# A transformer block on one core: where the shift of the attention scores stands in TensorE's order

## The chip, the cores and the metric

The kernel runs on one core of one Trainium2 chip. The metric is the device time of the whole program in microseconds (us). The engines are named as in the profile: PE (TensorE, matrix products), PEld (its weight loads), DVE (VectorE), ACT (ScalarE), POOL (GpSimd) and SP (SyncE, which only issues DMAs here).

## The reference

For a batch of 4 sequences of 2048 tokens with 512 features, the block normalises x and adds two branches to it, all in float32:

```
xn  = layernorm(x)
out = x + attention(xn) + ffn(xn)

attention: 16 heads of 32;  softmax(q k^T / sqrt(32)) v, then a projection
ffn:       the top 2 of 8 experts per sequence, chosen from token 0;
           mean over the two of  gelu(xn W1 + b1) W2 + b2
```

What matters here is the attention. For every head the scores are a 2048x2048 matrix. The softmax needs the largest score of each query, so that the exponential can be taken of score minus maximum.

## The kernel before, in words

**The unit of work.** Four heads (one group, `GH = 4`) stand beside each other on the 128 partitions: head j has its 32 features on partitions 32j to 32j+31. Work goes in units `U`, one for each combination of a sequence, a group of heads, a chunk of 512 queries (`qc`) and a tile of 128 keys (`kt`): 4 x 4 x 4 x 16 = 1024 units. Each unit makes transposed scores (128 keys by 512 queries) of the four heads.

**Two passes.** The maxima must be known before the exponentials. So the loop at lines 1044 to 1171 carries two passes at once: for unit U the second pass (shift, score, exponential, product with v), and for unit U + 22 (`LEAD`) the first pass, which computes the scores once more in the other orientation, for the maxima alone. The first 22 turns of the loop have only the first pass, the last 22 only the second.

**The products of a unit on PE**, each over 32 partitions (one head), into 128x512 float32, which is one PSUM bank:

- `shift` (lines 912 to 919): a bf16 product of a row of ones with the negated maxima, which stand split into three bf16 parts in `negm`. It starts the accumulation of the bank `s`. The loop calls it for all four heads at once.
- `score` (lines 921 to 928): the float32 product of keys and queries, which is accumulated on top of the shift in the same bank.
- `score_max` (lines 898 to 910): the float32 product of queries and keys for the maxima, into a bank `m`.

Because a product uses 32 of the 128 rows of the array, four products of four different heads (four row groups) can be under way at once. The loop orders the calls so that neighbours belong to different heads: shift 0 to 3, score 0 and 1, maxima 2 and 3, score 2 and 3, maxima 0 and 1. A float32 product is carried out as two passes, each with its own weight load; a bf16 product as one.

**What follows on the other engines.** ACT takes the exponential of the four `s` banks (line 1064) into the tile `p`; DVE takes the maxima of the four `m` banks (line 1071). POOL adds the tiles `p` up for the softmax's denominators (line 966). `p` has five buffers.

**What follows on PE.** After an even unit, `weigh` (line 937) multiplies the exponentials of the two units before with v. After most odd units come products of the dense layers (line 599): queries, keys and values of later groups, the two feed-forward layers, the projection. Which of them stands behind which unit is laid down by `Plan` (lines 41 to 303), together with the loads; some 50 odd units have none. Some units are followed by `add_keys` (line 972), which adds the denominators over the keys. All of these use all 128 rows and 32 columns of the array (`128*32` in the profile), while shift, score and maxima use 32 rows and 128 columns (`32*128`).

**PSUM.** All banks come from one pool of eight, `bank()` at line 345. They are handed out in the order of the program: a new product takes the bank that was asked for longest ago among those given back, and waits until its last reader has finished. Per unit eight banks are asked for, plus one for `acc` after an even unit and one or two for dense products after an odd one.

**The schedule is by hand** (`tc.manual_schedule()`): every engine executes its instructions in the order in which the Python code emits them.

Of the kernel before, what the change touches and what calls it, by code (L numbers as in the profile page):

```python
# [20 lines left out]
GH = P // HD  # L21
# [285 lines left out]
def block_kernel(  # L307
# [37 lines left out]
    def bank(name):  # L345
        return ps.tile([P, CH], F32, tag="bank", name=name)

    def rows_of(j):
        return slice(j * HD, (j + 1) * HD)
# [537 lines left out]
    def place(u):  # L887
        rest, kt = divmod(u, NT)
        rest, qc = divmod(rest, NCH)
        return (*divmod(rest, DC), qc, kt)  # L890
# [7 lines left out]
    def score_max(u, heads, tiles):  # L898

        b, g, qc, n = place(u)  # L900
        i, kc = divmod(n, NCH)
        if n == 0 and (b, g, qc) not in mx:
            mx[b, g, qc] = small.tile([P, GH, TPC, NCH], F32, tag="mx", name=f"mx_{b}_{g}_{qc}")
        for j in heads:
            t = bank(f"m{j}_{u}")
            r = rows_of(j)
            nc.tensor.matmul(  # L907
                t, qT[b, g, qc][r, ts(i, P)], kT[b, g, kc][r, :], start=True, stop=True
            )
            tiles.append((mx[b, g, qc][:, j, i, kc : kc + 1], t))  # L910

    def shift(u, heads, tiles):
        b, g, qc, kt = place(u)
        for j in heads:
            tiles[j] = bank(f"s{j}_{u}")
            r = rows_of(j)
            nc.tensor.matmul(  # L917
                tiles[j], ones_b[r, :], negm[b, g, qc][r, :], start=True, stop=False
            )

    def score(u, heads, tiles):
        b, g, qc, kt = place(u)
        for j in heads:
            r = rows_of(j)
            nc.tensor.matmul(  # L925
                tiles[j], kT[b, g, kt // TPC][r, ts(kt % TPC, P)], qT[b, g, qc][r, :],
                start=False, stop=True,
            )
# [115 lines left out]
    for U in range(-LEAD, plan.units):  # L1044
        second = U >= 0
# [3 lines left out]
        maxima, tiles = [], {}  # L1049


        if second:
            shift(U, range(GH), tiles)
        for h in range(2):
            if second:
                score(U, (2 * h, 2 * h + 1), tiles)
            if first_pass is not None:
                score_max(first_pass, (2 - 2 * h, 3 - 2 * h), maxima)


        if second:
# [111 lines left out]
    U = plan.units  # L1173
# [78 lines left out]
```

## Time and profile before

| | us |
|---|---|
| median of 3 runs (4901.69 to 4907.2) | 4903.32 |
| the profiled execution, device time | 4902.71 |
| its span, first to last instruction | 4900.9 |
| PE busy | 4860.0 (99%) |
| POOL busy | 4504.5 (92%) |
| DVE busy | 3761.9 (77%) |
| ACT busy | 2501.7 (51%) |
| granted TensorE clock, mean | 1.000 |

Three things help in reading it. PE's busy time is the union of products that overlap, and the end of each product is modelled, so 99% doesn't say that the array works at its peak; how far apart the starts of successive products lie says more. In the timeline `x4` joins neighbouring instructions of one kind. And a product can show as `32*128` (32 rows, 128 columns of the array) or `128*32`.

The costliest lines on PE are the products for `s` (line 925, 1926.1 us), `m` (line 907, 1916.8 us), `acc` (line 937, 985.3 us), the dense products (line 599), and the shifts (line 917, 412.7 us).

### The profile page before, as it was taken

Reading aid. Unit: us, or ns where it says so; the run is one execution under the profiler, and the core shown is the slowest. Engines: PE = TensorE matmul, PEld = TensorE weight load, DVE = VectorE, ACT = ScalarE, POOL = GpSimd, SP = SyncE. Lnnn points to the kernel's source line nnn. Section 1 sums busy time; section 2 is a strip of 40 time slices with the busy share of each in tenths; the row PEclk is TensorE's granted clock in tenths of the full one; section 3 lists DMA queues with packets and bytes.
Section 4 is the critical chain, followed back from the end, with each engine's and each line's share of the span. In section 5 each row is a group of like instructions: output and inputs, shape, how many; then the busy total and the mean of one; then the engine's idle time right before and its main releaser. Section 6 shows DMA issues by size and latency. Waiting matters only on the chain.

```text
span 4900.9 us, 112895 instructions
## 1 busy us (share of the span) xinstructions
PE 4860.0 (99%) x46860; PEld 1777.6 (36%) x46860; DVE 3761.9 (77%) x5979; ACT 2501.7 (51%) x4587; POOL 4504.5 (92%) x1524
## 2 busy tenths in 40 slices
PE   8999999999999999999999999999999999999999
PEld 2333333333434333333443443333343334333333
DVE  5777788777777788887777778887777777878772
ACT  1445456554454546564455455555545544555453
POOL 3899999999999998999999999999999999999994
PEclk9999999999999999999999999999999999999999
DMA  6434427654444654765454454476445465323322
GB/s 227 136 99 119 127 87 186 164 157 130 126 129 141 181 144 120 193 171 153 127 156 141 138 160 137 134 198 164 147 130 143 124 174 139 99 77 99 94 72 93
DMA packets 480963, 678.37 MB, mean 138 GB/s; under 512 B 145213, under 2 KB 287549, under 8 KB 463169
## 3 DMA queue, kind: packets, MB, share of 16 engines
q1 hardware_dynamic: 452512, 568.37, 36.5%
q0 software_dynamic: 27936, 102.77, 11.5%
q8 instruction: 369, 6.05, 0.5%
q14 instruction: 146, 1.19, 0.1%
HBM read 437.70 MB, written 193.46 MB: 129 GB/s over the span
## 4 chain that ended last, share of the span: by engine, by line
PE 87%; ACT 6%; POOL 4%; issue 1%; DVE 1%; DMA 1%; SPq 0%; POOLq 0%; DVEq 0%; ACTq 0%
PE acc L937 18%; PE s L925 16%; PE m L907 16%; PE ops L599 7%; PE qkps L599 7%; PE s L917 6%; PE hps L599 6%; PE vps L599 4%; PE prps L599 3%; POOL psum L966 3%; ACT p L1064 3%; PE keys L972 1%; ACT L836 1%; ACT L1068 1%; ACT h L1068 1%
## 5 line engine op out<-in xcount | busy, mean ns | idle before, releaser
L966 POOL TENSOR_TENSOR psum<-psum,p 128x2048 f32<-128x2048 f32 x819 | 3739.0, 4565 | 106.5 <-ACT p L1064 57.5
L1064 ACT ACTIVATE p<-s 128x512 f32<-128x512 f32 x4096 | 2117.9, 602 | 2132.2 <-PE m L907 1923.8
L1071 DVE TENSOR_REDUCE mx<-m 128x1 f32<-128x512 f32 x4096 | 2543.2, 683 | 567.1 <-PE m L907 564.1
L925 PE MATMUL s<-qT,kT 32*128 32x512 f32 x8192 | 1926.1, 587 | 0.0
L907 PE MATMUL m<-kT,qT 32*128 32x512 f32 x8192 | 1916.8, 590 | 0.5 <-DVE sacc L943 0.4
L907 PEld LDWEIGHTS m<-kT,qT 32*128 32x128 f32 x8192 | 923.0, 184 | 330.9 <-issue 240.6
L937 PE MATMUL acc<-p,v 128*32 128x512 f32 x8192 | 985.3, 598 | 16.2 <-ACT p L1064 11.7
L925 PEld LDWEIGHTS s<-qT,kT 32*128 32x128 f32 x8192 | 768.5, 185 | 30.2 <-issue 6.6
L937 PEld LDWEIGHTS acc<-p,v 128*32 128x32 f32 x8192 | 214.1, 109 | 714.7 <-ACT p L1064 402.0
L599 PE MATMUL ops<-wb_w,h 128*32 128x512 f32 x4096 | 466.0, 595 | 0.2 <-ACT p L1064 0.2
L946 DVE TENSOR_TENSOR sacc<-acc,sacc 128x512 f32<-128x512 f32 x448 | 309.8, 692 | 146.0 <-PE acc L937 146.0
L917 PE MATMUL s<-negms,ones_b 32*128 32x512 bf16 x4096 | 412.7, 384 | 6.2 <-ACT sums L984 2.5
L599 PE MATMUL hps<-xt,wt_w 128*32 128x512 f32 x3584 | 411.0, 596 | 0.0
L917 PEld LDWEIGHTS <-ones_b 32*128 32x128 bf16 x4096 | 105.6, 91 | 827.4 <-issue 820.6
L599 PE MATMUL qkps<-xt,wt_qk 128*32 128x512 f32 x3360 | 385.3, 596 | 0.3 <-ACT p L1064 0.3
L960 POOL TENSOR_TENSOR psum<-p,p 128x2048 f32<-128x2048 f32 x63 | 291.7, 4629 | 86.4 <-ACT p L1064 86.2
L599 PEld LDWEIGHTS ops<-wb_w,h 128*32 128x32 f32 x4096 | 120.0, 109 | 327.1 <-issue 229.8
L1087 DVE RECIPROCAL sums<-sums 128x128 f32<-128x128 f32 x252 | 236.1, 937 | 0.0
L599 PEld LDWEIGHTS hps<-xt,wt_w 128*32 128x32 f32 x3584 | 103.3, 109 | 288.6 <-issue 191.2
L801 DVE SCALAR_TENSOR_TENSOR row<-ops,row 128x512 f32<-128x512 f32 x128 | 88.5, 692 | 149.8 <-PE ops L599 143.1
L599 PEld LDWEIGHTS qkps<-xt,wt_qk 128*32 128x32 f32 x3360 | 96.9, 109 | 271.0 <-issue 179.2
L599 PE MATMUL vps<-wt_v,xt 128*32 128x256 f32 x2688 | 153.7, 381 | 0.0
(153 smaller groups left out, 2193.0 us busy)
## 6 DMA issues: line engine op xcount, KB each, us to landing
xt<-t_dram SPq DMA_DIRECT2D x203, 512.0 KB
xt<-xn_dram SPq DMA_DIRECT2D x151, 512.0 KB
psum<-p POOLq DMA_DIRECT2D x62, 1024.0 KB, 8.9
part_dram<-row SPq DMA_DIRECT2D x128, 256.0 KB
wt_w<-ws_dram SPq DMA_DIRECT2D x128, 128.0 KB
v<-v_dram SPq DMA_DIRECT2D x64, 256.0 KB
row<-part_dram SPq DMA_DIRECT2D x64, 256.0 KB
att_dram<-att SPq DMA_DIRECT2D x63, 256.0 KB
```

Of the source, the lines that this page charges most:

```text
L599: nc.tensor.matmul(pp[rows_of(j), :], lhsT[:, rows_of(j)], rhs, start=(first and n == 0), stop=(last and n == len(terms) - 1),)
L907: nc.tensor.matmul(t, qT[b, g, qc][r, ts(i, P)], kT[b, g, kc][r, :], start=True, stop=True)
L917: nc.tensor.matmul(tiles[j], ones_b[r, :], negm[b, g, qc][r, :], start=True, stop=False)
L925: nc.tensor.matmul(tiles[j], kT[b, g, kt // TPC][r, ts(kt % TPC, P)], qT[b, g, qc][r, :], start=False, stop=True,)
L937: nc.tensor.matmul(acc[r, :], held["v", (b, g, kt // TPC)][:, (kt + n) % TPC, r], pT[u + n][:, j, :], start=(n == 0), stop=(n == 1),)
L946: nc.vector.tensor_tensor(t, acc, t, ALU.add)
L960: nc.gpsimd.tensor_tensor(psums[b, g, qc], pT[u - 1], pT[u], ALU.add)
L966: nc.gpsimd.tensor_tensor(psums[b, g, qc], psums[b, g, qc], pT[u], ALU.add)
L1064: nc.scalar.activation(pT[U][:, j, :], tiles[j], AF.Exp, scale=SCALE)
L1068: nc.scalar.activation(flat, flat, AF.Gelu)
L1071: nc.vector.tensor_reduce(dst, t, AX.X, ALU.max, negate=True)
L1087: nc.vector.reciprocal(sums[before][:, q], sums[before][:, q])
```

## The change

The shift is no longer issued for all four heads ahead of the unit's other products. It is issued for two heads at a time: first for heads 0 and 1, then come the maxima products of heads 2 and 3, then the scores of heads 0 and 1; then the shift of heads 2 and 3, the maxima products of heads 0 and 1, and the scores of heads 2 and 3. No instruction is added or taken away on any engine; `shift`, `score` and `score_max` themselves are as they were.

```diff
-        if second:
-            shift(U, range(GH), tiles)
         for h in range(2):
             if second:
-                score(U, (2 * h, 2 * h + 1), tiles)
+                shift(U, (2 * h, 2 * h + 1), tiles)
             if first_pass is not None:
                 score_max(first_pass, (2 - 2 * h, 3 - 2 * h), maxima)
+            if second:
+                score(U, (2 * h, 2 * h + 1), tiles)
```

PE's order in a unit, by head (h shift, s score, m maxima):

```
before   h0 h1 h2 h3   s0 s1  m2 m3   s2 s3  m0 m1
after    h0 h1  m2 m3  s0 s1  h2 h3   m0 m1  s2 s3
```

As the eight banks of a unit are asked for in another order (before: s0 to s3, m2, m3, m0, m1; after: s0, s1, m2, m3, s2, s3, m0, m1), the products take over other banks from their predecessors, and the waits on ACT and DVE stand at other instructions. DVE takes the maxima in the same order of heads as before, 2, 3, 0, 1, and ACT the exponentials of heads 0 to 3.

## The prediction

> **What bounds the kernel now.** I read the page's busy times first, then the chain, then PE's rows among the costliest groups.
>
> ```profile
> PE 4860.0 (99%) x46860; PEld 1777.6 (36%) x46860; DVE 3761.9 (77%) x5979; ACT 2501.7 (51%) x4587; POOL 4504.5 (92%) x1524
> ...
> PE 87%; ACT 6%; POOL 4%; issue 1%; DVE 1%; DMA 1%; SPq 0%; POOLq 0%; DVEq 0%; ACTq 0%
> ...
> L925 PE MATMUL s<-qT,kT 32*128 32x512 f32 x8192 | 1926.1, 587 | 0.0
> ```
>
> PE is the bound: 99% busy, 87% of the chain, next to no idle time before its products. So the time is the sum of what PE's products take one after another, and the question is how a unit's 20 passes fit together. The timeline of one plain unit, with an `acc` behind it, shows that:
>
> ```profile
> 2001.76 0.61 PE L599 MATMUL ops<-wb_w,h 128*32 128x512 f32 x4
> 2002.31 0.40 PE L917 MATMUL s<-negms,ones_b 32*128 32x512 bf16 x4
> 2002.53 0.59 PE L925 MATMUL s<-qT,kT 32*128 32x512 f32 x2
> 2002.54 0.59 PE L907 MATMUL m<-kT,qT 32*128 32x512 f32 x2
> 2002.96 0.59 PE L925 MATMUL s<-qT,kT 32*128 32x512 f32 x2
> ...
> 2003.82 0.59 PE L907 MATMUL m<-kT,qT 32*128 32x512 f32 x2
> 2003.83 0.59 PE L925 MATMUL s<-qT,kT 32*128 32x512 f32 x2
> 2004.35 0.64 PE L937 MATMUL acc<-p,v 128*32 128x512 f32 x4
> ```
>
> Look at the starts. The four shifts start together at 2002.31; 0.22 us later the first passes of two scores and two maxima products start together; each float32 pass then takes 0.43 us (2002.53, 2002.96, ... 2003.82). Four of these steps follow, and 0.52 us after the last starts `acc` begins. From the first shift to `acc`: 0.22 + 3 x 0.43 + 0.52 = 2.04 us. Going through all starts in the trace, 980 of the 1002 units that have both passes stand alone between two `128*32` groups; 834 of them take 2.040 to 2.045 us, and all 980 together 2054.5 us. The other 22 stand in 11 pairs.
>
> Two gaps matter. After 2001.76 the next step would be due at 2002.19 but comes at 2002.31, and `acc` comes 0.09 us after 2003.83 + 0.43: PE empties when it changes between `128*32` and `32*128`. At such a change the weights of the first product cannot be loaded ahead either. What that costs shows in the 22 turns at the start that have maxima products only, so that float32 products come first after the change:
>
> ```profile
> 54.05 1.14 PE L907 MATMUL m<-kT,qT 32*128 32x512 f32 x8
> 55.12 0.64 PE L599 MATMUL vps<-wb_v,xq_stage 128*32 128x512 f32 x4
> ```
>
> Two steps of 0.43 us take 54.05 to 55.12 = 1.07 us: 0.21 us over, of which 0.10 us is the emptying as above. The remaining 0.11 us is the float32 weight load that nothing hides. In the unit at 2002.31 there is no such loss: bf16 shifts come first, the second pass starts after 0.22 us, and the float32 loads run under the shift.
>
> **The change part by part.** Call heads 0 and 1 group A, heads 2 and 3 group B. Group A keeps its order: shift, score, maxima. Group B goes from shift, maxima, score to maxima, shift, score.
>
> Do A and B run independently? In before they march in step, so the change needs it. A unit whose maxima products wait for a bank answers:
>
> ```profile
> 986.62 0.40 PE L917 MATMUL s<-negms,ones_b 32*128 32x512 bf16 x4
> 986.85 0.59 PE L925 MATMUL s<-qT,kT 32*128 32x512 f32 x2
> 987.04 0.70 PE L907 MATMUL m<-kT,qT 32*128 32x512 f32 x2
> 987.28 0.59 PE L925 MATMUL s<-qT,kT 32*128 32x512 f32 x2
> 987.58 0.72 PE L907 MATMUL m<-kT,qT 32*128 32x512 f32 x4
> 988.00 0.59 PE L925 MATMUL s<-qT,kT 32*128 32x512 f32 x2
> ```
>
> Group B's maxima products start 0.19 us late, at 987.04, and their second passes at 987.58; group A goes on at 986.85 and 987.28 undisturbed, and its own maxima products (in the x4) start before s2 and s3 at 988.00, though the program has them after. So the groups run independently and out of program order. The 0.70 against 0.59 is again the open load: 987.04 to 987.58 is 0.54, not 0.43.
>
> Group B's new sequence: maxima first, load open: 0.54, then 0.43; shift; two score passes. For the shift in the middle the trace has a place, too: where two units with scores only stand side by side, four shifts come at 4823.06, in the same mode, and the scores behind them at 4823.27.
>
> ```profile
> 4822.20 1.02 PE L925 MATMUL s<-qT,kT 32*128 32x512 f32 x8
> 4823.06 0.38 PE L917 MATMUL s<-negms,ones_b 32*128 32x512 bf16 x4
> 4823.27 1.02 PE L925 MATMUL s<-qT,kT 32*128 32x512 f32 x8
> ```
>
> Before it 2 x 0.43, the shift itself 0.21 to 0.22, loads hidden on both sides. So B's last pass starts at 0.01 + 0.54 + 0.43 + 0.22 + 0.43 = 1.62 us after the unit's start (before: 1.52), and the unit takes 1.62 + 0.52 = 2.14 us instead of 2.04: +0.10 us. Bounds: 0.09 (shift at 0.21) to 0.11. Group A ends at 1.94, as before, and waits. Over the 980 units, raising all below 2.141 us to that: 834 x 0.10 and a little = +83.5 us.
>
> The Trainium skill speaks against the change more strongly: "TensorE: Matmul & The Clock Gate", Part 3, has matmuls start and end strictly in program order. The rows at 987.58 and 988.00 contradict it. If it held, s0 and s1 could not start before m3's second pass at 0.55 us; A would end about 0.3 us later and the whole would cost some 270 us, an estimate.
>
> The waits that move are all on banks; nothing else on any queue moves, no DMA, nothing on SP's or POOL's queues. The program of after shows which reader each product now waits for.
> (a) `acc` and the dense product waited for the exponential of s0 of the same unit, now for the maximum of m2, which DVE has earlier than 2.14 us. In 57 units a late ACT (a gelu and its table load) held them, at 2.34 us on average; down to 2.141 this gives −11 us.
> (b) 35 units like the one at 986.62 (2.334 us, `keys` directly before): m2 waited for the exponential of s3. Now m0 does, which comes 0.9 us later; m3 waits for the reduce of m0, some 0.05 us. 35 x (2.334 − 2.19) = −5 us.
> (c) The 11 pairs (5.365 us, two units with nothing between): DVE's four maxima take 2.48 us from 1.25 on (1.36 in before). The second unit's shift of head 1 waits for the second of them, 2.55, the shift of head 3 for the fourth, some 3.8; then 0.22 + 0.43 + 0.52, about 5.0 us: −4 us.
> (d) 49 units wait for DVE to free a dense bank for m1 or m0. These now stand ahead of s2 and s3, which wait with them; but the wait ends at the same moment and two float32 steps follow either way: the longer of 2.14 and what they take now, 0.
> The plain unit keeps its cover: in the unit at 2002.31 DVE adds up the dense result (line 801) from 0.13 to 0.82 us after the start, m1's bank is free at 0.88, and m1 and s2 need it at 0.9 to 1.0. If DVE came 0.1 us later, that would cost up to 0.1 us a unit.
>
> POOL (92%) and DVE get 0.1 us more per unit and are not pushed. Sum: 83.5 − 11 − 5 − 4 = +63 us. The profiled execution took 4902.7 us (span 4900.9, 1.8 around it), 0.6 below the median: 4902.7 + 63 = 4966 us. Its own range: 0.09 us a unit and twice the gain on waits, 75 − 40, to 0.11 and no gain, 94: 4938 to 4997.
>
> **The rivals.** More loads open: B's bf16 load and the float32 load of s2 behind it have never run beside float32 passes of the other group in step; the pairs show both hidden, but there all groups are in step. A second open load is another 0.11 us x 834: 4966 + 90 = about 5056. Groups only partly independent (the out-of-order window too short for B's longer queue) would lie above, to 5150. For: two more waits stand ahead of s2. Against: 4823.06. Chance 0.14.
> Faster: PE brings m2's load in before the change of mode is over. Then a unit stays at 2.04 us and only the waits count, down to 2.04: about −16, −10, −5, so 4872. It decides if B's first maxima passes are 0.43 apart instead of 0.54. Against: at 54.05 it is never so. Chance 0.08.
> No change: the load is open but half covered, or the waits gain far more than counted: within 10 us. Chance 0.04.
>
> **How the numbers follow.** Likeliest (0.74): 4966. The range 4940 to 5055 takes in nearly all of it and most of the second-load case; left out are the window too short, no change and faster. Faster or slower is counted from 0.2%, 10 us, about what a measurement can tell: faster 0.08, same 0.04, slower 0.88.
>
> **What would show it.** Right: plain units at 2.14 us; L907's first passes in B at 0.69 instead of 0.59; B's shifts 0.97 us after A's; the mean of L907 up from 590 to about 616 ns (2 of 8 passes by 105 ns); `acc` no longer released by ACT. Wrong: units at 2.04 (load hidden), or at 2.25 and more (a second load open, or m2's passes holding s0 back).

## The result and the profile after

The kernel after takes 4947.07 us (median of 4 runs, 4945.27 to 4949.49) against 4902.5 us before (median of 4 as well): a ratio of 1.0084, 95% interval 1.0072 to 1.0096. It is slower by 0.8%, about 44.6 us, where +63 was forecast; the stated range, 4940 to 5055, holds it. The profiled execution has a span of 4945.5 us.

The page of after, its busy times, its chain and PE's rows among the costliest groups:

```profile
PE 4922.2 (100%) x46860; PEld 1977.4 (40%) x46860; DVE 3763.5 (76%) x5979; ACT 2500.7 (51%) x4587; POOL 4505.0 (91%) x1524
...
PE 96%; POOL 2%; DMA 1%; issue 1%; DVE 1%; ACT 0%; SPq 0%; POOLq 0%; DVEq 0%; ACTq 0%
...
L907 PE MATMUL m<-kT,qT 32*128 32x512 f32 x8192 | 2144.2, 615 | 0.5 <-ACT p L1064 0.4
L925 PE MATMUL s<-qT,kT 32*128 32x512 f32 x8192 | 2017.9, 588 | 0.0
```

No engine does more work; POOL, DVE and ACT are busy as long as before. PE's share of the chain rises from 87% to 96% and ACT's falls from 6% to 0%: PE became longer in itself, and waited less for ACT. The mean of a maxima product rose from 590 to 615 ns; 616 was foretold for two open loads in eight passes.

The timeline of a plain unit of after, from its first shift to the dense product behind it:

```profile
2007.98 0.39 PE L917 MATMUL s<-negms,ones_b 32*128 32x512 bf16 x2
2007.98 0.70 PE L907 MATMUL m<-kT,qT 32*128 32x512 f32 x2
2008.20 0.59 PE L925 MATMUL s<-qT,kT 32*128 32x512 f32 x2
2008.51 0.59 PE L907 MATMUL m<-kT,qT 32*128 32x512 f32 x2
2008.63 0.59 PE L925 MATMUL s<-qT,kT 32*128 32x512 f32 x2
2008.94 0.38 PE L917 MATMUL s<-negms,ones_b 32*128 32x512 bf16 x2
2009.06 0.59 PE L907 MATMUL m<-kT,qT 32*128 32x512 f32 x2
2009.16 0.59 PE L925 MATMUL s<-qT,kT 32*128 32x512 f32 x2
2009.49 0.59 PE L907 MATMUL m<-kT,qT 32*128 32x512 f32 x2
2009.59 0.59 PE L925 MATMUL s<-qT,kT 32*128 32x512 f32 x2
2010.11 2.35 PE L599 MATMUL ops<-wb_w,h 128*32 128x512 f32 x20
```

The two groups of heads can be read apart. Group A (0 and 1): shift 2007.98, scores 2008.20 and 2008.63, maxima 2009.06 and 2009.49, each step 0.43 us. Group B (2 and 3): maxima at 2007.98 with 0.70 instead of 0.59, their second pass 0.53 us later at 2008.51, the shift at 2008.94, scores at 2009.16 and 2009.59. B ends 0.10 us after A, and the unit takes 2.13 us.

The weight loads (PEld) of the same unit say what the longer first pass is made of:

```profile
2007.98 0.19 PEld L907 LDWEIGHTS m<-kT,qT 32*128 32x128 f32 x2
2007.99 0.19 PEld L925 LDWEIGHTS s<-qT,kT 32*128 32x128 f32 x2
2008.09 0.19 PEld L907 LDWEIGHTS m<-kT,qT 32*128 32x128 f32 x2
2008.20 0.19 PEld L925 LDWEIGHTS s<-qT,kT 32*128 32x128 f32 x2
```

Group A's first load runs under the shift, and the load for its second pass starts as soon as the first pass does, at 2008.20. Group B's second load starts only at 2008.09, 0.11 us after its first pass is shown to start: by the same 0.11 us that this pass is longer.

What `acc` waits for, in the list of waits of before and, in the second fence, of after (engine, line, releaser: us in total, times, longest):

```profile
PEld acc L937 <- ACT p L1064: 402.0, 505, 3.8
```

```profile
PEld acc L937 <- DVE mx L1071: 380.0, 500, 1.0
```

Most of each total is the ordinary gap between weight loads, some 0.8 us each time. What changed is who is named, and the longest wait: `acc` no longer stands behind ACT.

The unit behind `keys` that stood at 986.62 in before no longer has a gap in group B, whose second maxima pass follows 0.53 us after the first:

```profile
992.27 0.39 PE L917 MATMUL s<-negms,ones_b 32*128 32x512 bf16 x2
992.28 0.70 PE L907 MATMUL m<-kT,qT 32*128 32x512 f32 x2
992.50 0.59 PE L925 MATMUL s<-qT,kT 32*128 32x512 f32 x2
992.81 0.59 PE L907 MATMUL m<-kT,qT 32*128 32x512 f32 x2
```

Taking every unit of the two traces by its place in the order gives the account below. "Plain" are the units that took under 2.06 us in before.

| units | before, us | after, us | change | forecast |
|---|---|---|---|---|
| 835 plain | 1704.4 | 1785.7 | +81.3 | +83.5 |
| 59 held at their end, by ACT | 144.0 | 127.5 | −16.5 | −11 |
| 35 behind `keys` alone | 81.7 | 74.8 | −6.9 | −5 |
| 11 pairs | 60.3 | 55.2 | −5.1 | −4 |
| 47 waiting for a dense bank | 112.4 | 106.9 | −5.5 | 0 |
| 4 waiting at a shift | 11.9 | 8.9 | −3.1 | 0 |
| all else | 2740.8 | 2741.3 | +0.5 | 0 |
| sum | | | +44.7 | +63 |

### The profile page after: what moved, and what is told of

The parts are those of the page before. It is cut to its first block, busy times and chain, and to the rows that moved or that the text cites. A ratio compares the mean times of both kernels' runs of the same rounds, so it can differ in the third digit from the quotient of the medians.

```text
span 4945.5 us, 112895 instructions
## 1 busy us (share of the span) xinstructions
PE 4922.2 (100%) x46860; PEld 1977.4 (40%) x46860; DVE 3763.5 (76%) x5979; ACT 2500.7 (51%) x4587; POOL 4505.0 (91%) x1524
## 4 chain that ended last, share of the span: by engine, by line
PE 96%; POOL 2%; DMA 1%; issue 1%; DVE 1%; ACT 0%; SPq 0%; POOLq 0%; DVEq 0%; ACTq 0%
PE m L907 26%; PE acc L937 18%; PE ops L599 9%; PE s L925 8%; PE s L917 8%; PE hps L599 8%; PE qkps L599 8%; PE vps L599 4%; PE prps L599 3%; POOL psum L966 2%; PE keys L972 1%; DVE mx L1071 0%; PE kps L599 0%; DMA psum<-p 0%; PE qps L599 0%
## 5 line engine op out<-in xcount | busy, mean ns | idle before, releaser
L907 PE MATMUL m<-kT,qT 32*128 32x512 f32 x8192 | 2144.2, 615 | 0.5 <-ACT p L1064 0.4
L925 PE MATMUL s<-qT,kT 32*128 32x512 f32 x8192 | 2017.9, 588 | 0.0
L907 PEld LDWEIGHTS m<-kT,qT 32*128 32x128 f32 x8192 | 848.1, 183 | 107.7 <-issue 21.5
L917 PE MATMUL s<-negms,ones_b 32*128 32x512 bf16 x4096 | 786.6, 379 | 4.8 <-DVE mx L1071 2.1
L917 PEld LDWEIGHTS <-ones_b 32*128 32x128 bf16 x4096 | 198.7, 92 | 942.0 <-issue 813.2
L599 PE MATMUL prps<-wt_p,xt_at 128*32 128x256 f32 x2688 | 153.8, 380 | 0.0
```

The source lines that it names most:

```text
L599: nc.tensor.matmul(pp[rows_of(j), :], lhsT[:, rows_of(j)], rhs, start=(first and n == 0), stop=(last and n == len(terms) - 1),)
L907: nc.tensor.matmul(t, qT[b, g, qc][r, ts(i, P)], kT[b, g, kc][r, :], start=True, stop=True)
L917: nc.tensor.matmul(tiles[j], ones_b[r, :], negm[b, g, qc][r, :], start=True, stop=False)
L925: nc.tensor.matmul(tiles[j], kT[b, g, kt // TPC][r, ts(kt % TPC, P)], qT[b, g, qc][r, :], start=False, stop=True,)
```

## The experiments

The theory: the time is lost in the float32 weight load with which group B begins behind the change of mode, once per unit; and some comes back because the eight banks pass on in another order, so that `acc` and the dense products wait for DVE's first maximum instead of ACT's first exponential. Two things were changed at once, the place of the shift and the order of the products behind it, so the first two runs take them apart. The ratios are to the kernel before as measured again beside each run: 4906.02 us for the first four runs, 4904.88 us for the last two.

**All shifts first, maxima ahead of the scores.** Against before:

```diff
         if second:
             shift(U, range(GH), tiles)
         for h in range(2):
-            if second:
-                score(U, (2 * h, 2 * h + 1), tiles)
             if first_pass is not None:
                 score_max(first_pass, (2 - 2 * h, 3 - 2 * h), maxima)
+            if second:
+                score(U, (2 * h, 2 * h + 1), tiles)
```

> The shift is issued for all four heads first again; only the order of the products behind it is that of after (maxima of heads 2 and 3, scores of 0 and 1, maxima of 0 and 1, scores of 2 and 3). Theory (after loses time because in heads 2 and 3 a float32 weight load stands open behind the change of mode, and it gains some back because banks pass on in another order, so that acc and the dense products wait for DVE's first maximum instead of ACT's first exponential): no load is open, plain units 2.04 us, the waits of after stay away; 4866 us, between 4855 and 4885, faster than before. Rival (what costs is that maxima products stand ahead of the scores): as after, about 4947 us.

Measured: 4903.18 us, ratio to before 0.9995 (0.9986 to 1.0004). Neither number came. The loss is gone: plain units are at 2.041 us (median) and the mean of a maxima product is back at 590 ns, so maxima ahead of scores don't cost a plain unit anything. The units held by ACT fall from 144.0 to 122.8 us, as the theory has it. But the 35 units behind `keys` rise from 81.7 to 94.7 us, 2.71 us each, which I had not seen coming. One of them in this kernel's timeline:

```profile
1205.91 0.56 PE L917 MATMUL s<-negms,ones_b 32*128 32x512 bf16 x4
1206.70 0.70 PE L907 MATMUL m<-kT,qT 32*128 32x512 f32 x2 [0.23 <-DVE mx L1071]
1206.71 0.70 PE L925 MATMUL s<-qT,kT 32*128 32x512 f32 x2
```

Behind the shifts everything, the scores too, waits for DVE's maximum of the unit before and starts 0.79 us after the first shift, where 0.23 us is usual. With all four shifts in front, the first maxima product gets the bank of the last maximum, and the scores stand behind it. So the new order of the products doesn't by itself bring these units the gain that after shows.

**The shift split, scores ahead of the maxima.** Against after:

```diff
             if second:
                 shift(U, (2 * h, 2 * h + 1), tiles)
+                score(U, (2 * h, 2 * h + 1), tiles)
             if first_pass is not None:
                 score_max(first_pass, (2 - 2 * h, 3 - 2 * h), maxima)
-            if second:
-                score(U, (2 * h, 2 * h + 1), tiles)
```

> The shift is split in two as in after, but the products behind it keep the order of before: shift 0 and 1, scores 0 and 1, maxima 2 and 3, shift 2 and 3, scores 2 and 3, maxima 0 and 1. Heads 2 and 3 again begin with a float32 load. Theory: plain units 2.135 us as in after, but banks pass on as in before, so the waits on ACT stay: 4902 + 81 and a little less for stalled units, 4970 to 4985 us, slower than after. Rival (maxima ahead of the scores are what costs): about 4903 us.

Measured: 4973.59 us, ratio 1.0137 (1.0122 to 1.0153), inside what the theory gave and 70 us from the rival. Plain units take 2.149 us, though the program has the scores first: the groups are independent, so group B still begins with its float32 load. The units held by ACT stay at 140.0 us, and the list of waits names ACT again (the exponential is line 1063 in this kernel):

```profile
PEld acc L937 <- ACT p L1063: 393.4, 504, 3.5
```

With the first run this settles both halves: the split makes the unit longer, whatever stands behind it; the order of the products decides whether `acc` waits for ACT. It also says what the units behind `keys` and the pairs owe to which: here, with the old order of the products, they take 75.3 and 55.4 us, as good as in after (74.8 and 55.2). Their gain comes with the split, which lets the first maxima product take its bank after two shifts instead of four.

**All heads in step, maxima first.** The body of the loop becomes:

```diff
+        if first_pass is not None:
+            score_max(first_pass, (2, 3, 0, 1), maxima)
+        if second:
+            shift(U, range(GH), tiles)
+            score(U, range(GH), tiles)
```

> All four heads in step: maxima of all four, then the shift of all four, then the scores of all four. No bf16 product runs beside a float32 one of another head, but every head begins with an open float32 load. Theory (the open load costs, once per unit): plain units 2.135 us as in after; the exponentials come about 1 us later, which a few units may feel; 4940 to 4970 us. Rival (what costs is that the two pairs of heads run out of step, bf16 beside float32): plain units 2.04 us, 4870 to 4905 us.

Measured: 5002.43 us, ratio 1.0198 (1.0182 to 1.0213). On the disputed point the theory holds: nothing runs out of step here and yet plain units take 2.145 us.

```profile
2030.45 1.14 PE L907 MATMUL m<-kT,qT 32*128 32x512 f32 x8
2031.41 0.39 PE L917 MATMUL s<-negms,ones_b 32*128 32x512 bf16 x4
2031.63 1.04 PE L925 MATMUL s<-qT,kT 32*128 32x512 f32 x8
```

Maxima at 2030.45, shift 0.96 us later: 0.53 + 0.43, the open load again. The total lies above the expected range, and 55 us above after. Of these, 27.6 us come from the units behind `keys` (102.4 us, 20.7 more than before), 10.0 from the pairs (4.8 more than before) and 15.3 from the plain units, of which a few took up to 3.3 us.

**One head late.** Shift 0, 1 and 2 first, shift 3 where after has shift 2 and 3:

```diff
+        if second:
+            shift(U, (0, 1, 2), tiles)
+        if first_pass is not None:
+            score_max(first_pass, (2, 3), maxima)
+        if second:
+            score(U, (0, 1), tiles)
+            shift(U, (3,), tiles)
+        if first_pass is not None:
+            score_max(first_pass, (0, 1), maxima)
+        if second:
+            score(U, (2, 3), tiles)
```

> Only head 3 gets its shift late: shift 0, 1 and 2, maxima 2 and 3, scores 0 and 1, shift 3, maxima 0 and 1, scores 2 and 3. Theory (the four row groups run independently and the last one sets the end of the unit): one open load costs as much as two, plain units 2.135 us, 4940 to 4955 us. Rival (each open load costs its own share): half, plain units 2.09 us, 4900 to 4912 us.

Measured: 4977.73 us, ratio 1.0147 (1.0132 to 1.0163): the total is outside both, again by the units behind `keys` (98.4 us against 74.8 in after). Plain units take 2.139 us, so one open load costs as much as two. In the start of one, a maxima product of one head has the 0.69, and the single late shift comes 0.98 us after the others:

```profile
2018.61 0.39 PE L917 MATMUL s<-negms,ones_b 32*128 32x512 bf16 x3
2018.63 0.69 PE L907 MATMUL m<-kT,qT 32*128 32x512 f32 x1
2018.84 0.59 PE L925 MATMUL s<-qT,kT 32*128 32x512 f32 x2
...
2019.59 0.37 PE L917 MATMUL s<-negms,ones_b 32*128 32x512 bf16 x1
```

The mean of a maxima product counts the open loads: 590 ns with none, 602 with one, 615 with two, 639 with four; the plain unit takes 2.041, 2.139, 2.136 (2.149 with the scores first) and 2.145 us. The last row group to finish sets the end, and it doesn't matter how many are late with it.

**The split only where it helps.** The first experiment's kernel, with the order of after in the even units whose predecessor has no dense products (the cut starts from that kernel):

```diff
+        quiet = U > 0 and U % 2 == 0 and U - 1 not in plan.items
-        if second:
+        if second and not quiet:
             shift(U, range(GH), tiles)
         for h in range(2):
+            if quiet:
+                shift(U, (2 * h, 2 * h + 1), tiles)
             if first_pass is not None:
```

> All four shifts first and maxima ahead of scores, as in the first experiment, except in the even units whose predecessor has no dense products behind it (35 behind keys alone, 11 second units of pairs): these take the order of after, with the shift split. Theory (in those units the four shifts in front stand in line for banks that ACT and DVE still read, and splitting lets the rest go ahead; everywhere else the split only opens a load): from the first experiment the 35 units fall from 2.71 to 2.14 us, -20 us, the pairs from 5.76 to 5.0 us, -8 us: 4875 us, between 4865 and 4885, faster than before and than after. Rival (the stall behind keys comes from the order in which the banks pass on, which is kept): about 4903 us.

Measured: 4882.62 us, ratio to before 0.9953 (0.9939 to 0.9966). It is the fastest of all, 22 us under before and 64 under after. The gain on before is that of the ACT-held units (122.8 us against 144.0); what the other groups gain and lose cancels. The units behind `keys` came down from 94.7 to 80.8 us only, not to 74.8: at 2.31 us, one maxima product still starts 0.19 us late. It waits for DVE's maximum of head 0 in the unit before, which ends 0.13 us after the unit's start here and 0.09 us before it in after. The pairs take 56.5 us.

**The split there alone**, with everything else as before (scores ahead of maxima in the other units):

```diff
-        if second:
+        quiet = U > 0 and U % 2 == 0 and U - 1 not in plan.items
+        if second and not quiet:
             shift(U, range(GH), tiles)
         for h in range(2):
-            if second:
+            if quiet:
+                shift(U, (2 * h, 2 * h + 1), tiles)
+            elif second:
                 score(U, (2 * h, 2 * h + 1), tiles)
             if first_pass is not None:
                 score_max(first_pass, (2 - 2 * h, 3 - 2 * h), maxima)
+            if quiet:
+                score(U, (2 * h, 2 * h + 1), tiles)
```

> The kernel before, with the order of after in those same 46 units only. Theory: the 35 units fall from 2.33 to 2.14 us, -7 us, the pairs from 5.48 to 5.0 us, -5 us; acc still waits for ACT in the others, as in before: about 12 us less than before, 4888 to 4897 us. Rival (the gains belong to the order of the banks in all units, not to these units): as before.

Measured: 4897.94 us, ratio 0.9985 (0.9976 to 0.9995), 7 us under before and just above the range of the theory. In the trace the units behind `keys` give 4.5 us and the pairs 3.0, less than the 7 and 5 expected. Of the 35 units, 29 do take 2.14 us; five take 2.26, and one takes 3.93, held by DVE, which had itself waited for a DMA (`xn_dram`, until 990.50). Everything else took 5 us more in the profiled execution, most of it at the start and the end of the program. That execution was the slowest of the eleven (4900.17 us), and nothing shown here ties the 5 us to the edit.

## Why the prediction was right

**The open load** was the main term and the right one. 2.14 us a unit was foretold from three places in the trace of before, 2.136 measured (median); +83.5 us foretold, +81.3 measured. It is shown, not only argued: the loss goes with the split in either order of the products, stays when all heads run in step, and doesn't grow with the number of heads. Two of the prediction's sums are 0.01 us off as printed (0.22 + 3 x 0.43 + 0.52 is 2.03, and 0.01 + 0.54 + 0.43 + 0.22 + 0.43 is 1.63), because each step is rounded; the starts in the traces give 2.041 us for the unit of before and 1.62 us for the last pass of after.

**The independence of the row groups** held. Group A kept its times, and the second run showed the same 0.1 us with the program's order of maxima and scores reversed. Against the rule of the Trainium skill that was weighed ("TensorE: Matmul & The Clock Gate", Part 3), the unit shown above has B's second maxima pass at 2008.51 and A's first score at 2008.20, though the program has both passes of the maxima first.

**The second load** of the first rival didn't open: B's shift starts 0.43 us after its second maxima pass (2008.51, 2008.94), the scores 0.22 us after it.

**The gain on waits** was the term that was mis-sized: −20 us forecast, −37 measured, which is nearly all of the distance from +63 to +44.7. It has several parts. Point (a) gave −16.5 instead of −11, because I had sorted units by the first thing that was late in them: four units with an average of 3.7 us waited for a dense bank first and then for ACT as well (1.47 us in two of them, 0.99 and 0.12 in the others), and I had put them under (d), which was to change by nothing. They gave 5.0 of the 16.5 us. Point (d) itself gave −5.5: the prediction said that DVE gets 0.1 us more per unit, and didn't draw the consequence that the banks it frees might come earlier. That this is the cause is not shown. The medians of these 47 units speak for it in part: 2.30 us in before, 2.31 in the two runs with plain units of 2.04 us and maxima first, 2.22 in after, 2.24 with one head late, 2.29 with the split and the scores first. But they take 2.32 with all heads in step, where the plain unit is 0.1 us longer too. The four units that wait at a shift gave 3.1 us, which I had left out. Of these, 2.1 come from one unit (at 990.81 in before), which stood behind DVE while DVE waited for a DMA. It is free of this wait in every other kernel, also in the last one, where its own order is that of before and a DMA into the same tensor (`xn_dram`) holds the neighbouring unit of 3.93 us instead. So this part is not shown to belong to the change, and may be chance. Points (b) and (c) were 2 and 1 us too small; in (c) the 5.365 us hold for ten of the eleven pairs, while the first took 6.64 us in before and gave 0.8 us by itself.

**The reading behind (b)** was incomplete: it named which reader each product waits for, but not that the number of shifts in front of the maxima decides which bank a maxima product gets, and with the order of the products what else is held up. Most of the first experiment's miss of 37 us comes from that: the units behind `keys` and the pairs took 28 us more than in after.

One sentence of the description ahead of the prediction has to be corrected: a bank passes on in the order in which the last products of the banks stand in PE's program, not in the order in which the banks were asked for. In before, where the two orders differ, the waits of the program follow the first: at 987.04 the maxima product of head 2 starts 0.05 us after the exponential of head 3 has ended, while the maximum it would otherwise wait for had ended 0.8 us before. The waits named in the prediction were read from the programs themselves and are not touched.

## What to carry to other kernels

When the array changes between tile shapes, the first product behind the change pays for its weight load (here 0.1 us for float32, 0.01 us for bf16); put the product with the cheapest load first in every row group, as the bf16 shift was before. An order written by hand decides two things at once, what runs beside what and which buffer passes to whom, and they can be had separately: the best kernel here takes the old place of the shift, but for 46 units, and the new order of the products. And before calling a stalled unit unchanged, follow it to its end: the first thing that is late need not be what it waits for longest.

## What the runs showed of the hardware

- Products in different row groups start out of program order: in before by up to 0.3 us (maxima products of heads 0 and 1 at 987.71, the scores of heads 2 and 3, ahead of them in the program, at 988.00), and bf16 beside float32 costs neither anything (plain steps of 0.43 us and 0.22 us in after, where they overlap).
- The load of the second pass in the same row group is hidden behind the first pass (0.19 us of load within a step of 0.43 us). Behind a change between `128*32` and `32*128` the first load stands open, 0.10 to 0.11 us for a 32x128 float32 load, and 0.01 us for a bf16 one: from a shift to the score behind it 0.226 us pass there, 0.216 us in the middle of a unit of after. It also stands open behind a wait for a bank (0.70 instead of 0.59 at 987.04 in before).
- The cost of an open load doesn't add up over row groups: 1, 2 or 4 of them lengthen the unit by 0.10, 0.10 (0.11 with the scores first) and 0.10 us.
